# Moving two of four key and value projections from the prologue into the steps of a fused graph attention layer

## The chip, the core and the metric

The kernel runs on one core of a Trainium2 chip. The metric is the device time of one execution in microseconds (us), lower is better. TensorE (PE) multiplies, VectorE (DVE) and ScalarE (ACT) work element by element, GpSimd (POOL) adds and issues accumulating transfers, and SyncE (SP) issues most of the other transfers. Each engine works through its own instructions in their order.

## The reference, cut to what matters

Eight graphs (F) of 2048 nodes (N) with 256 channels (C) share one adjacency matrix. Every graph goes through attention with 8 heads of 32 channels, masked by the adjacency, then two layer norms around a feed-forward part, and an outer residual with a third layer norm.

```python
def layer(x, adj, w_qkv, ...):                       # x: (8, 2048, 256), adj: (2048, 2048) int32
    q, k, v = split(einsum('fnc,ck->fnk', x, w_qkv)) # 8 heads of 32 channels each
    scores = einsum('fnhd,fmhd->fhnm', q, k) / sqrt(32)
    scores = where(adj > 0, scores, -1e9)
    attn = softmax(scores, axis=-1)
    t = einsum('fhnm,fmhd->fnhd', attn, v)
    x = layernorm(x + t) * g1 + b1
    f = relu(x @ w1 + b1_) @ w2 + b2_
    return layernorm(x + f) * g2 + be2

out = layernorm(x + layer(x, adj, ...))
```

All matrix products are in float32.

## The kernel before, in words

**Tiling.** The heads are two groups (g) of four. Queries come in four chunks of 512 (qc), keys and values in 16 blocks of 128 (mb), which lie in four column chunks (c) of 512. One *item* is (f, qc, g, mb): the scores of four heads, 512 queries and 128 keys. There are 8 x 4 x 2 x 16 = 1024 items in that nesting, and the main loop in `fast_path` takes one *step* for each. In step t it first calls `advance(t)`, then records the exponential of item t+1 (L283), the scores of item t+2 (L276 on TensorE, then two adds of the mask from PSUM on VectorE, L279), and the product with the values of item t (L310). So on TensorE a step is: one piece of fill work, one group of scores, one group of values. `add_up` sums the exponentials of a query chunk on POOL, in part by additions (L339) and in part by accumulating transfers (L336).

**Fill work.** Everything else is written as generators that stop at `yield BANK` or `yield MORE` before each unit of TensorE work. `start(t, generator, due)` enters one into the list `fill`, which is kept in order of due step. `advance` resumes them by that order, as a credit for TensorE time allows; a generator past its due step goes on regardless. The fill jobs that matter here are:

- `turn(f, c)` loads a chunk of x of the next graph (L200), transposes it on TensorE (L95), and stores it to DRAM (`XD`, L205).
- `project(f, c, g)` makes the keys and values of one column chunk and one head group. It reloads the transposed chunk from `XD` (`reload`, L224) unless it is handed to it, multiplies on TensorE (L54, keys in two units, values in two), and copies the results on ScalarE (L217 and L243).
- `ask(f, c)` makes the queries of chunk c for both groups (L54, four units).
- `mask_job(n)` makes one block of the mask for query chunks 2 and 3. It loads two blocks of int32 adjacency (L156), casts them on ScalarE (L161), transposes them on TensorE (L168), encodes them on VectorE (L170), and stores the result to DRAM (L172). There are 16 such jobs; their buffers are those of one spare key and value pair and of `turned`, `hT` and `y`. `load_mask` (L179) brings mask blocks back for every query chunk.
- `denominator` (L382), `outcome`, `tail` and `feed_forward` finish a query chunk.

The tables `NEXT` and, for the first graph, `LATER` give the step within a graph at which such jobs are started. The reloads and turns share a pool of three buffers, `ld` (tile name `in`).

**Prologue.** `begin()` runs ahead of the steps. It takes the four column chunks for query chunk 0 and then for query chunk 1. For each it converts the adjacency chunk on VectorE (L696) and turns it into mask blocks (`mask_blocks`: 16 transposes on TensorE, L141, then one half copied by ScalarE, L147, the other by VectorE, L145, each stored by SP, L148). In the first four rounds it also transposes x (L95) and projects the keys and values of group 0; in the last four it projects those of group 1. In the end it records the scores of items 0 and 1:

```python
elif qc == 1:
    yield from project(0, c, 1, xT)
...
yield from mask_blocks(qc, c, cv, ...)
if (qc, c) == (1, NCK - 1):
    for k in range(LEAD):
        scores(items[k])
    exponentials(items[0])
```

The order of all instructions on every engine is fixed when the program is recorded; only waits on semaphores act at run time.

Of the kernel before, what the change touches and what calls it, by code (L numbers as in the profile page):

```python
# [61 lines left out]
def fast_path(ctx, tc, cst, x, adj, out, RS):  # L62
    nc = tc.nc
    F, N, C = x.shape
    NCK, TPC, MB = N // CH, CH // P, N // P
# [68 lines left out]
    def mask_blocks(qc, mc, cv, to=None):  # L134
        for half in range(2):
            yield BANK
            ps = bank(BF16)
            for r in range(2):
                for j in range(TPC):
                    rr = 2 * half + r  # L140
                    nc.tensor.transpose(ps[:, r, j * P:(j + 1) * P], cv[:, j, rr * P:(rr + 1) * P], identb)  # L141
            k = 2 * mc + half
            m = to[half] if to else mask_piece(0, qc, k)
            if half:
                nc.vector.tensor_tensor(m, ps, cst["ones"][:, 0:1, None].to_broadcast([P, 2, CH]), ALU.min, saturate=False)  # L145
            else:
                nc.scalar.copy(m.bitcast(I8), ps)  # L147
            nc.sync.dma_start(MD[qc, k], words(m))  # L148
# [133 lines left out]
    def exponentials(item):  # L282
        nc.scalar.activation(PT[item], PT[item], AF.Exp, scale=1.0 / math.sqrt(D))  # L283
# [371 lines left out]
    LEAD = 2  # L655
# [3 lines left out]
    def ask(f, c):  # L659
# [5 lines left out]
            60: [(project, 1, 0)], 66: [(ask, 3)], 72: [(turn, 3)], 80: [(project, 2, 0)], 98: [(ask, 0)], 100: [(project, 3, 0)],  # L665
            104: [(project, 0, 1)], 108: [(project, 1, 1)], 112: [(project, 2, 1)], 116: [(project, 3, 1)]}

    LATER = {80: [], 100: [(project, 2, 0)], 104: [(project, 3, 0)], 108: [(project, 0, 1)], 112: [(project, 1, 1)],
             116: [(project, 2, 1)], 120: [(project, 3, 1)]}

    def begin():
        todo = deque((qc, c) for qc in range(2) for c in range(NCK))
        rows, cols = [], deque()

        def fetch():
            if todo:
                qc, c = todo.popleft()
                t = pp.tile([P, 4, CH], F32, name="p").bitcast(I32)
                nc.sync.dma_start(t, adj[qc * CH:(qc + 1) * CH, c * CH:(c + 1) * CH].rearrange("(j p) m -> p j m", p=P))
                cols.append((qc, c, t))  # L680

        for c in range(NCK):
            rows.append(pp.tile([P, 4, CH], F32, name="p"))
            xc = rows[c][:, 0:2, :].rearrange("p a (b c) -> p (a b) c", c=C)
            nc.sync.dma_start(xc, x[0, c * CH:(c + 1) * CH, :].rearrange("(j p) c -> p j c", p=P))
            fetch()
        fetch()
        while cols:
            qc, c, col = cols.popleft()
            if c % 2 == 0:  # L690
                two = pp.tile([P, 4, CH], F32, name="p").rearrange("p a q -> p (a q)").bitcast(BF16)
            cv = two[:, c % 2 * TPC * CH:(c % 2 + 1) * TPC * CH].rearrange("p (j m) -> p j m", m=CH)

            for half, what in enumerate((CODE, MASKED)):
                part = slice(half * 2 * P, (half + 1) * 2 * P)
                nc.vector.tensor_scalar(cv[:, :, part], col[:, :, part], 0.0, what, op0=ALU.is_le, op1=ALU.mult)  # L696
            fetch()
            xT = rows[c][:, 2:4, :]
            if qc == 0:
                yield from turn_rows(rows[c][:, 0:2, :].rearrange("p a (b c) -> p (a b) c", c=C), xT)  # L700
                nc.sync.dma_start(XD[0][c], xT)
                XT[0, c] = xT
                if c == 0:
                    yield from queries(0, 0, xT)
                yield from project(0, c, 0, xT)
            elif qc == 1:
                yield from project(0, c, 1, xT)
            if qc and c % 2 == 0:
                out4 = take([P, 4, 2, CH], F8)
                give(out4)  # L710
            yield from mask_blocks(qc, c, cv, [out4[:, c % 2 * 2 + i] for i in range(2)] if qc else None)
            if (qc, c) == (1, NCK - 1):
                for k in range(LEAD):
                    scores(items[k])
                exponentials(items[0])

    for _ in begin():
        pass
    state["side"] = 0
    n_mask = 0  # L720
    spare.append(([kp.tile([P, CH], F32, name="kT"), vp.tile([P, TPC, P], F32, name="v").rearrange("p j c -> p (j c)")], FRAME))
    for pool, name, until in ((work, "turned", 41), (work, "hT", 41), (yp, "y", 56)):
        both = pool.tile([P, 2, CH], F32, name=name)
        spare.append(([both[:, a, :] for a in range(2)], until))
    for t, (f, qc, g, mb) in enumerate(items):
        if g == 1 and mb % 2 and (f + 1 < F or qc + 1 < NCK):
            t0 = t
            while ((qc + 1) % NCK, mb // 2) not in MADE:
                advance(t0, finish=True)
                t0 += 1  # L730
            load_mask(f + (qc + 1) // NCK, (qc + 1) % NCK, mb // 2)
        while n_mask < MB and t >= 2 + 3 * n_mask:
            start(t, mask_job(n_mask), 3 * MB - 2 + 2 * n_mask if n_mask < MB // 2 else 4 * MB - 2 + 2 * n_mask)
            n_mask += 1
        for what, *which in (NEXT if f else {**NEXT, **LATER}).get(t % FRAME, []):
            to = f if what is ask and which[0] else f + 1
            if to < F:
                at = (0, 0, 0) if what is turn else (which[0], 0, 0) if what is ask else (0, which[1], which[0] * TPC)
                start(t, what(to, *which), t + 3 * MB if what is turn else items.index((to, *at)) - LEAD - 1)
        if t == len(items) - 2 * MB - 6:  # L740
            state["xb"] = take([P, TPC, C], F32)
            nc.sync.dma_start(state["xb"], x[f, qc * CH:(qc + 1) * CH, :].rearrange("(p j) c -> p j c", p=P))
        if t == len(items) - MB:
            xr, xb = state["rows"] = [take([P, TPC, C], F32) for _ in range(2)]
            nc.sync.dma_start(xr.rearrange("p (h j) c -> p h j c", h=2),
                              x[f, qc * CH:(qc + 1) * CH, :].rearrange("(h p j) c -> p h j c", h=2, p=P))
        if t == len(items) - MB + 6:
            nc.gpsimd.tensor_tensor(xb, xr, rows(cst["be2r"]), ALU.add)
        if t:
            advance(t)  # L750

        if t + 1 < len(items):
            exponentials(items[t + 1])
        if t + LEAD < len(items):
            nf, _, ng, nmb = items[t + LEAD]
            t0 = t
# [256 lines left out]
```

## Time and profile before

| | us |
|---|---|
| median of three runs | 3171.28 |
| lowest and highest run | 3169.4 and 3172.4 |
| the profiled execution | 3170.48 |
| span of the profile | 3168.7 |
| TensorE busy | 3075.1 (97%) |
| VectorE busy | 2752.2 (87%) |
| POOL busy | 2592.1 (82%) |
| ScalarE busy | 2424.2 (77%) |
| first value product (step 0) starts at | 68.16 |
| value product of step 151 starts at | 517.53 |

The span runs from the first to the last instruction in the trace; the profiled execution's own time adds what lies around it. A busy TensorE is not one at its peak, since its instructions overlap and their ends are modelled; the start times of successive value products are the better ruler. The granted TensorE clock is 0.99 on average over the span. The timeline gives for each merged row: start, duration, engine, line, operation, tiles, count, and in brackets the idle time before it and what ended it.

### The profile page before, as it was taken

The numbers are of one execution on the slowest core, as the hardware profiler recorded it, in microseconds if no ns is written. First come the engines' busy times: TensorE is split into PE (matmuls) and PEld (weight loads), VectorE is DVE, ScalarE is ACT, GpSimd is POOL, SyncE is SP. The second block draws the span as 40 slices with busy tenths as digits, with TensorE's granted clock in tenths as the row PEclk, the third lists the DMA queues.
The fourth block names the chain that finished last, engine by engine and source line by source line (L and its number), as shares of the span: only waits on it lengthen the run. The fifth ranks groups of instructions, "written<-read, shape, count | busy, mean of one in ns | idle before, by whom it ended". The sixth has DMA issues, their size and how long they took to land.

```text
span 3168.7 us, 68994 instructions
## 1 busy us (share of the span) xinstructions
PE 3075.1 (97%) x29220; PEld 970.7 (31%) x29220; DVE 2752.2 (87%) x3138; ACT 2424.2 (77%) x1934; POOL 2592.1 (82%) x1358
## 2 busy tenths in 40 slices
PE   7999999999999999999999999999999999999986
PEld 4223233323333233323233323323233233332223
DVE  4989888988888998888988888888888888889885
ACT  4877778777778877778777878777778777778774
POOL 1768888888888888889888888888889788889885
PEclk9999999999999999999999999999999999999998
DMA  7998888888889888789878889879879788888861
GB/s 251 210 218 195 181 184 192 190 193 193 178 178 205 191 188 180 169 196 221 183 167 186 189 202 195 176 176 204 190 173 208 174 193 193 176 176 165 175 148 42
DMA packets 165467, 586.89 MB, mean 185 GB/s; under 512 B 15360, under 2 KB 84480, under 8 KB 116512
## 3 DMA queue, kind: packets, MB, share of 16 engines
q0 software_dynamic: 63696, 430.60, 68.9%
q1 hardware_dynamic: 100640, 150.50, 14.1%
q8 instruction: 231, 3.78, 0.5%
q10 hardware_dynamic: 816, 1.31, 0.1%
q14 instruction: 84, 0.69, 0.1%
HBM read 146.15 MB, written 37.75 MB: 58 GB/s over the span
## 4 chain that ended last, share of the span: by engine, by line


## 5 line engine op out<-in xcount | busy, mean ns | idle before, releaser
L279 DVE TENSOR_TENSOR p<-s,mask 128x1024 f32<-128x1024 f32 x2016 | 2371.5, 1218 | 305.9 <-PE s L276 173.4
L283 ACT ACTIVATE p<-p 128x2048 f32<-128x2048 f32 x1024 | 1955.8, 1910 | 568.4 <-DVE p L279 465.5
L339 POOL TENSOR_TENSOR p<-p 128x2048 f32<-128x2048 f32 x378 | 1846.0, 4884 | 336.7 <-ACT p L283 336.3
L276 PE MATMUL s<-qT,kT 32*128 32x512 f32 x8064 | 1154.7, 642 | 48.4 <-DVE p L279 44.5
L310 PE MATMUL x<-p,v 128*32 128x512 f32 x8064 | 1076.5, 606 | 3.5 <-ACT oT L314 3.5
L276 PEld LDWEIGHTS s<-qT,kT 32*128 32x128 f32 x8064 | 315.9, 183 | 655.6 <-DVE p L279 628.6
L336 POOL DMA_DIRECT2D p<-p x378 | 407.5, 1079 | 69.5 <-ACT p L283 41.4
L310 PEld LDWEIGHTS x<-p,v 128*32 128x32 f32 x8064 | 158.7, 108 | 770.8 <-issue 307.1
L382 PE MATMUL x<-p,halves 128*32 128x512 f32 x2016 | 261.1, 592 | 0.3 <-ACT turned L575 0.3
L54 PE MATMUL x<-in,wqkv 128*32 128x512 f32 x1888 | 245.6, 592 | 1.5 <-DVE y L170 0.8
L360 ACT ACTIVATE y<-y,nb,rs 128x256 f32<-128x256 f32 x372 | 218.3, 591 | 2.5 <-POOL nb L357 2.5
L348 DVE BATCH_NORM_STATS2 st<-y 128x6 f32<-128x256 f32 x372 | 154.9, 416 | 0.0
L54 PE MATMUL x<-turned,w1s 128*32 128x512 f32 (+1 forms) x1024 | 126.9, 593 | 0.3 <-ACT in L194 0.3
L54 PEld LDWEIGHTS x<-wqkv,in 128*32 128x32 f32 x3584 | 102.2, 110 | 62.9 <-issue 54.5
L54 PE MATMUL x<-w2s,hT 128*32 128x256 f32 x2016 | 120.3, 379 | 0.0
L54 PE MATMUL x<-wqkv,in 128*32 128x128 f32 x3584 | 117.1, 273 | 0.0
L382 PEld LDWEIGHTS x<-p,halves 128*32 128x32 f32 x2016 | 65.4, 110 | 149.8 <-issue 147.8
L54 PEld LDWEIGHTS x<-in,wqkv 128*32 128x32 f32 x1888 | 61.1, 110 | 143.4 <-issue 114.8
L354 POOL TENSOR_TENSOR rs<-rs,mhalf 128x4 f32<-128x4 f32 x93 | 96.4, 1036 | 7.8
L441 POOL TENSOR_TENSOR y<-y,g2r 128x1024 f32<-128x1024 f32 x31 | 100.5, 3241 | 0.0
L443 POOL TENSOR_TENSOR y<-y,be2r 128x1024 f32<-128x1024 f32 x30 | 92.3, 3076 | 0.6
L54 PEld LDWEIGHTS x<-w2s,hT 128*32 128x32 f32 x2016 | 65.5, 110 | 68.9 <-issue 35.6
(155 smaller groups left out, 1426.0 us busy)
## 6 DMA issues: line engine op xcount, KB each, us to landing
p<-p POOLq DMA_DIRECT2D x380, 1024.0 KB, 10.1
in<-xd SPq DMA_DIRECT2D x87, 512.0 KB, 8.5
mask<-md SPq DMA_DIRECT2D x248, 128.0 KB, 8.7
y<-in_x_dram POOLq DMA_DIRECT2D x60, 512.0 KB, 9.9
out_dram<-y SPq DMA_DIRECT2D x31, 512.0 KB, 6.2
in<-in_x_dram SPq DMA_DIRECT2D x30, 512.0 KB, 10.2
xd<-in SPq DMA_DIRECT2D x28, 512.0 KB, 8.6
p<-in_adj_dram SPq DMA_DIRECT2D x8, 1024.0 KB, 13.5
```

The costliest lines, as they stand in the source:

```text
L54: nc.tensor.matmul(out[r:r + D], lhsT[:, r:r + D], rhs, start=start, stop=stop)
L276: nc.tensor.matmul(ps2[half][:, j, :], KT[f, mb // TPC, g][r:r + D, (mb % TPC) * P:(mb % TPC + 1) * P], QT[f, qc, g][r:r + D, :], start=Tr ...
L279: nc.vector.tensor_tensor(pt[:, 2 * half:2 * half + 2, :], ps, MK[f, qc, mb // 2][:, mb % 2, None, :].to_broadcast([P, 2, CH]), ALU.add)
L283: nc.scalar.activation(PT[item], PT[item], AF.Exp, scale=1.0 / math.sqrt(D))
L310: nc.tensor.matmul(O[grp][r:r + D, :], V[f, mb // TPC, g][:, mb % TPC, r:r + D], PT[item][:, h, :], start=(mb == 0), stop=(mb == LAST))
L336: nc.gpsimd.dma_start(PT[f, qc, g, chain[0]], PT.pop(item), accum_op=ALU.add)
L339: nc.gpsimd.tensor_tensor(first, first, PT.pop(item), ALU.add)
L348: nc.vector.bn_stats(st, t[:, j, :])
L354: nc.gpsimd.tensor_tensor(rs, rs, cst["mhalf"], ALU.pow)
L360: nc.scalar.activation(t[:, j, :], t[:, j, :], AF.Identity, bias=nb[:, j:j + 1], scale=rs[:, j:j + 1])
L382: nc.tensor.matmul(ps[r:r + D, :], cst["halves"][:, g, :], term[:, h, :], start=(n == 0), stop=(n == len(blocks) - 1))
L441: nc.gpsimd.tensor_tensor(z, z, rows(cst["g2r"]), ALU.mult)
```

## The change

The change has five parts, all of which act in the first graph.

1. In the first four rounds of the prologue, the mask blocks of a chunk are recorded after the projection of the next chunk (`behind`).
2. Of the four group 1 projections, the first two stay in the prologue. Those of chunks 2 and 3 become fill jobs, started at step -6, with due steps 21 and 25.
3. The scores of items 0 and 1 and the first exponential are recorded ahead of the mask blocks of the last chunk (query chunk 1, c = 3).
4. The queries of chunk 1, `ask(0, 1)`, are started at -6 instead of step 2.
5. The due steps of the mask jobs of query chunk 3 are seven later, and the loads of its masks for the first graph are recorded eight steps later (`wanted`).

```diff
-    LATER = {80: [], 100: [(project, 2, 0)], ...
+    LATER = {2: [], 80: [], 100: [(project, 2, 0)], ...
...
                 if c == 0:
                     yield from queries(0, 0, xT)
                 yield from project(0, c, 0, xT)
-            elif qc == 1:
+                yield from behind
+                behind = mask_blocks(qc, c, cv)
+                continue
+            yield from behind
+            behind = ()
+            if c < 2:
                 yield from project(0, c, 1, xT)
-            if qc and c % 2 == 0:
+            if c % 2 == 0:
                 out4 = take([P, 4, 2, CH], F8)
                 give(out4)
-            yield from mask_blocks(qc, c, cv, [out4[:, c % 2 * 2 + i] for i in range(2)] if qc else None)
-            if (qc, c) == (1, NCK - 1):
+            yield from mask_blocks(qc, c, cv, [out4[:, c % 2 * 2 + i] for i in range(2)])
+            if c == NCK - 2:
                 for k in range(LEAD):
                     scores(items[k])
                 exponentials(items[0])
+                for k in (2, 3):
+                    start(-6, project(0, k, 1), MB + TPC * k - LEAD - 1)
+                start(-6, ask(0, 1), 2 * MB - LEAD - 1)
+                advance(-6)
...
         if g == 1 and mb % 2 and (f + 1 < F or qc + 1 < NCK):
+            wanted.append((t + (8 if (f, qc) == (0, 2) else 0), f + (qc + 1) // NCK, (qc + 1) % NCK, mb // 2))
+        while wanted and wanted[0][0] <= t:
+            _, *which = wanted.popleft()
             t0 = t
-            while ((qc + 1) % NCK, mb // 2) not in MADE:
+            while tuple(which[1:]) not in MADE:
                 advance(t0, finish=True)
                 t0 += 1
-            load_mask(f + (qc + 1) // NCK, (qc + 1) % NCK, mb // 2)
+            load_mask(*which)
         while n_mask < MB and t >= 2 + 3 * n_mask:
-            start(t, mask_job(n_mask), 3 * MB - 2 + 2 * n_mask if n_mask < MB // 2 else 4 * MB - 2 + 2 * n_mask)
+            start(t, mask_job(n_mask), 3 * MB - 2 + 2 * n_mask if n_mask < MB // 2 else 4 * MB + 5 + 2 * n_mask)
```

`advance(-6)` lets the three jobs run up to their first wait, which records their three reloads of transposed x (L224) on SP's queue. Their TensorE work follows from step 1 on. The rest of the kernel is as before.

More of the change, by code (lines that the diff above doesn't have):

```diff
@@ L666, in fast_path @@
             104: [(project, 0, 1)], 108: [(project, 1, 1)], 112: [(project, 2, 1)], 116: [(project, 3, 1)]}
-    LATER = {80: [], 100: [(project, 2, 0)], 104: [(project, 3, 0)], 108: [(project, 0, 1)], 112: [(project, 1, 1)],
+    LATER = {2: [], 80: [], 100: [(project, 2, 0)], 104: [(project, 3, 0)], 108: [(project, 0, 1)], 112: [(project, 1, 1)],
              116: [(project, 2, 1)], 120: [(project, 3, 1)]}
@@ L672, in begin @@
         todo = deque((qc, c) for qc in range(2) for c in range(NCK))
-        rows, cols = [], deque()
+        rows, cols, behind = [], deque(), ()
         def fetch():
@@ L719, in fast_path @@
     state["side"] = 0
-    n_mask = 0
+    n_mask, wanted = 0, deque()
     spare.append(([kp.tile([P, CH], F32, name="kT"), vp.tile([P, TPC, P], F32, name="v").rearrange("p j c -> p (j c)")], FRAME))
```

## The prediction

> **What bounds the kernel now.** I read the page first, then the timeline of the first 80 us, the windows around the gap I found there, the timeline step by step up to 520 us, and the DMA view of one late transfer.
>
> ```profile
> PE 3075.1 (97%) x29220; PEld 970.7 (31%) x29220; DVE 2752.2 (87%) x3138; ACT 2424.2 (77%) x1934; POOL 2592.1 (82%) x1358
> PE   7999999999999999999999999999999999999986
> ```
>
> TensorE is busy all through, except in the first slice of 79 us and at the end. The change touches only the first 520 us: in the built programs (compared by order, not run) every TensorE step from step 152 on holds the same work before and after. So I price the prologue and 151 steps.
>
> ```profile
> 54.17 1.92 PE L54 MATMUL x<-p,wqkv 128*32 128x512 f32 x16
> 55.91 1.93 PE L54 MATMUL x<-wqkv,p 128*32 128x128 f32 x64
> 57.78 1.07 PE L141 MATMUL s<-identb,p 128*128 128x128 bf16 x16
> 58.88 1.23 DVE L145 TENSOR_TENSOR in<-s,ones 128x1024 fp8e5<-128x1024 bf16 x1 [2.17 <-PE s L141]
> 60.16 1.14 PE L276 MATMUL s<-qT,kT 32*128 32x512 f32 x8 [1.32 <-DVE in L145]
> 61.42 2.35 DVE L279 TENSOR_TENSOR p<-s,mask 128x1024 f32<-128x1024 f32 x2 [1.32 <-PE s L276]
> 62.70 2.09 PE L276 MATMUL s<-qT,kT 32*128 32x512 f32 x8 [1.40 <-DVE p L279]
> 68.16 1.94 PE L310 MATMUL x<-p,v 128*32 128x512 f32 x8
> 72.04 1.07 PE L310 MATMUL x<-p,v 128*32 128x512 f32 x8
> ```
>
> These are the last quarter of the prologue and the start of the steps (columns: start, duration, engine, line, operation). The projection of one column chunk holds TensorE from 54.17 to 57.78, 3.61 us; the mask turn takes 1.0; then scores and mask adds alternate between TensorE and VectorE. The first value product (step 0) starts at 68.16, the second at 72.04. The score group of 60.16 took 1.14 us and that of 62.70 took 2.09: half clock. The windows show the clock (last three columns: granted clock, DMA share, GB/s):
>
> ```profile
> 58.85:61.85 3.00, 1.14 (x8) 0.31 (x8) 1.65 (x2) 0.59 (x1) 0.00 (x0) 1.00 0.36 93
> 61.85:72.05 10.20, 8.00 (x33) 1.76 (x34) 6.64 (x6) 5.19 (x3) 0.00 (x0) 0.50 1.08 294
> ```
>
> Three us with 1.14 us of work, and the clock is halved for 10.2 us.
>
> In the steps, the distance from one value product to the next depends on the fill work between:
>
> ```profile
> 79.56 1.07 PE L310 MATMUL x<-p,v 128*32 128x512 f32 x8
> 82.05 1.06 PE L310 MATMUL x<-p,v 128*32 128x512 f32 x8
> ...
> 87.63 1.06 PE L310 MATMUL x<-p,v 128*32 128x512 f32 x8
> 88.51 1.04 PE L54 MATMUL x<-in,wqkv 128*32 128x512 f32 x8
> ...
> 90.55 1.06 PE L310 MATMUL x<-p,v 128*32 128x512 f32 x8
> ```
>
> An empty step takes 2.49 (VectorE's two mask adds, 2 x 1.22, are the limit; TensorE's own work is 1.07 + 0.88 = 1.95). A step with one unit of projection or row sum takes 2.92: TensorE is the limit, and the unit adds 0.975. A step with a transpose of x takes 2.65. A mask turn (L168, then 1.21 on VectorE at L170) takes 2.62, and the step after it 3.26 to 3.39.
>
> One step stands out, the 32nd, 5.43 us:
>
> ```profile
> 142.24 1.58 SPq L156 DMA_DIRECT2D kT<-in_adj_dram  x1
> 159.56 0.62 ACT L161 CAST kT<-kT 128x512 bf16<-128x512 int32 x1 [2.44 <-DMA kT<-in_adj_dram]
> 162.52 0.16 PEld L310 LDWEIGHTS x<-p,v 128*32 128x32 f32 x8 [3.56 <-ACT oT L314]
> ```
>
> An adjacency load was 17.3 us on its way, ScalarE stood on its cast for 2.44 us, and the exponential, queued behind the cast, was late. The DMA view of 139.4 to 144.5 says why:
>
> ```profile
> q0 software_dynamic: 125, 1.02, 102.1%
> q1 hardware_dynamic: 231, 0.20, 12.2%
> ```
>
> POOL's accumulating transfers (q0) fill the engines while they run, and SP's loads (q1) land in bunches after them.
>
> **What the Trainium skill says.** "TensorE: Matmul & The Clock Gate", What's actually happening: an idle window of about 3.4 us halves the clock and a busy window restores it. The trace agrees with the halving (0.50 above) and needs some 5 us of work without a gap (67 to 72) to come back. "DMA: Bandwidth & Descriptors", Anatomy of one DMA: waiting is done by the issuing sequencer, so a DMA that waits holds up all behind it on its queue; the long SP gap before 100.12 shows it. Same page, Issuing engines are not separate DMA queues: all queues share the 16 engines; the 102.1% and 12.2% agree.
>
> **The change, part by part.**
>
> (1) Mask turns of the first four chunks go behind the next chunk's projection. TensorE stood still from 17.2 to 20.7 for the first adjacency block. In its place it now waits for x chunk 1, which landed at 1.78 + 19.3 = 21.07, against 22.07 when that chunk's transposes started. The 1.0 of the mask turn is paid later, partly at full clock. I take -0.3 (0 to -1).
>
> (2) Two projections leave the prologue: 2 x 3.61 = 7.2 us off TensorE. But the new order on VectorE is: mask add of quarter 2, mask adds of items 0 and 1, conversion of quarter 3 (L696), its L145, then item 2. Followed with the durations above: the turn of (1,1) ends at 49.3; L145 50.6; L696 (1.28) 51.85; second half of the turn 52.4; L145 53.7; half a score group 54.4; mask add 56.8; next 59.2; L696 60.5; half a turn, 62.1 at half clock; L145 63.4; scores of item 2 at half clock 65.5. There step 0 starts, against 68.16. TensorE works only about 1.8 of the 6.9 us from 53 on, so I take the halved clock. Step 1 then follows at 65.5 + 1.9 (values) + 1.6 (a unit, partly at half clock) + 1.1 = 70.1, against 72.04: **-1.9**. At full clock throughout it would be 66.4, -5.6; at half clock to the end 72, 0.
>
> (3) The steps. From step 1 to step 151 the kernel before took 517.53 - 72.04 = 445.5. Afterwards steps 2 to 151 hold eight units more on net (a projection is two units for keys and two for values): 8 x 0.975 = +7.8. Steps without fill are 2, 3, 4, 5, 14, 16, 23, 28 to 31 and 80 before, and 23, 28 to 31 and 76 to 79 after: three fewer, each hiding 2.49 - 1.95 = 0.54, -1.6. Taking the steps one at a time at the durations above gives another -1.3, since four mask turns in a row (steps 44 to 47, then 4.03) become three. Sum **+4.9** (1.5 to 6.5), with the 2.2 us of step 32 (5.43 against 3.26) left in.
>
> (4) SP's queue. Three loads of transposed x are now issued ahead of the last two mask stores; the third (for the queries) takes the buffer of the first and so waits until TensorE has read it for the values, in step 3 to 4, about 77.8. Queued behind it: two mask stores, all eight adjacency loads (issued at 61.6 to 68.2 before) and the next graph's x. The first adjacency load is then issued near 79.2; landing takes 5.9 with POOL quiet, 85, and ScalarE wants it before item 8's exponential, near 86.4. It just fits, cost 0 (0 to 3). Stores and mask reloads have ten steps or more; nothing.
>
> (5) The mask jobs that follow are one to five steps later. POOL's transfers around 140 to 167 keep their times, as step 20 falls at 125.9 in both. The job whose cast stood at 159.5 has successors: the load for job 8 is now issued behind the store of transposed x, which landed at 165.56, so it lands near 167.5; ScalarE wants it at 164.8. With some of that hidden by the exponential's lead I take **+2.0** (0 to 5). The later due times and the reloads of the last query chunk's masks eight steps later leave one mask that depends on a store issued near step 102 and is wanted at step 108, 17 us for a store and a load (median 8.7): 0 (0 to 3).
>
> (6) Copies for keys, values and queries move with their units; ScalarE has 0.5 to 1 us free per step there; nothing. The query projection (0,1) moves from steps 7 to 10 to 9 to 12; same price.
>
> Sum: -1.9 + 4.9 + 2.0 = **+5.0** on the profiled execution's 3170.5 us (span 3168.7), 3175.5. The median of the runs is 0.8 above the profiled time, so 3176.3.
>
> **Rivals.** A, the forecast: the saved TensorE time is largely replaced by the VectorE chain, and the units come back in the steps; +5, from -1 to +10 with the bounds of (2), (3) and (5), 3170 to 3181.
>
> B, slower: the adjacency loads. If job 8's load lands after one more of POOL's transfers (their landings are 5.5 to 7.6 apart: 153.8, 159.3, 166.9), ScalarE stands that much longer; +5.5, in all +10.5, 3182. It decides from a landing later than about 170 us. For it: loads in this stretch took 16 to 17 us already. Against it: when ScalarE stands, POOL's transfers stop too, and SP's catch up.
>
> C, faster: the clock stays full (-5.6) and the wait of step 32 goes (-2.2) with no new one: -5.6 + 4.9 - 2.2 = -2.9, and with -1 in (1), 0.7 less, and the low end of (3), 3.4 less, -7.0: 3164 to 3168. For it: the score groups break the idle time. Against it: before, 1.14 us of work in 3 us did not keep the clock.
>
> D, that the projections don't move or drift to their due times: the built order has them in steps 1 to 8; excluded.
>
> **How the numbers follow.** A 0.53, B 0.24, C 0.23. The bound of 0.2% is 6.3 us, about what a measurement of this kernel can tell. A's spread puts 0.32 within it and 0.21 above; B lies above; C puts 0.15 below and 0.08 within. Faster 0.15, same 0.40, slower 0.45: A, the likeliest case, sits just inside the bound. The range 3166 to 3186 leaves out the far ends of B and C.
>
> **What would show it.** Step 0 near 65.5 and step 1 near 70 with a clock of 0.50 before them show (2); steps 2 to 12 at 2.92 show (3); SP's third load of transposed x near 78 and the first adjacency load just behind show (4); ScalarE standing on L161 near 159 and 165 shows (5). Step 1 before 68 speaks for C, a stand of over 4 us on L161 for B. If step 151 comes with the difference of step 1 unchanged, (3) is wrong.

## The result, and the profile after

The changed kernel takes 3187.29 us in the median of six runs (3183.81 to 3189.53), the kernel before 3170.76 beside it (3168.36 to 3172.4). The ratio is 1.0054, 95% interval 1.0044 to 1.0064: slower by 17 us, where 5 were forecast. The profiled execution took 3187.07, with a span of 3185.2 against 3168.7, so +16.5.

The page hides it. Its busy times and its TensorE slices read nearly as before:

```profile
PE 3081.9 (97%) x29220; PEld 972.8 (31%) x29220; DVE 2752.4 (86%) x3138; ACT 2424.0 (76%) x1934; POOL 2591.8 (81%) x1358
PE   7899999999999999999999999999999999999986
```

Half a per cent doesn't show in 40 slices of 80 us. The ruler that shows it is the start of each step's value product (L310), step by step, in the two timelines; below, step n is the time from the value product of step n-1 to that of step n. The difference, after minus before, is +2.49 at step 0, +2.25 at step 1, +4.26 at step 7, +10.73 at step 9, +10.85 at step 31, +13.79 at step 34 and +17.31 at step 151. From there on the work is the same and 0.8 comes back by the end.

Timeline of the changed kernel, end of the prologue (start, duration, engine, line, operation, in brackets the idle time before it):

```profile
51.12 0.62 PE L141 MATMUL s<-identb,p 128*128 128x128 bf16 x8
...
55.35 3.46 PE L276 MATMUL s<-qT,kT 32*128 32x512 f32 x8
...
65.42 1.89 PE L141 MATMUL s<-identb,p 128*128 128x128 bf16 x16 [3.14 <-DVE p L696]
68.63 2.09 PE L276 MATMUL s<-qT,kT 32*128 32x512 f32 x8 [1.32 <-DVE in L145]
70.65 1.79 PE L310 MATMUL x<-p,v 128*32 128x512 f32 x8
...
74.29 1.06 PE L310 MATMUL x<-p,v 128*32 128x512 f32 x8
```

The mask turn (the transposes at L141) of query chunk 1 and column chunk 1, below (1,1), starts at 51.12 (48.58 before). From there to step 0 takes 19.53 us, against 19.58 before: no gain, although two projections have left. Its windows (TensorE busy first, granted clock third from the end) show why: the clock is halved from 55 us on.

```profile
54.00:56.00 2.00, 1.90 (x18) 1.41 (x20) 1.19 (x3) 1.01 (x1) 0.00 (x0) 0.77 0.22 72
...
60.00:64.00 4.00, 2.09 (x8) 0.52 (x8) 2.87 (x4) 1.91 (x1) 0.00 (x0) 0.50 0.31 126
```

The largest loss is between steps 7 and 9. Timeline of the changed kernel, SP's queue:

```profile
57.09 25.39 SPq L224 DMA_DIRECT2D in<-xd  x3
82.53 0.90 SPq L148 DMA_DIRECT2D md<-in  x2
83.47 0.49 SPq L156 DMA_DIRECT2D kT<-in_adj_dram  x1
```

The three reloads form one row of 25 us: the third is issued only at 82.16, two mask stores follow, and the first adjacency load leaves at 83.47. The view of SP's waits (us in total, times, longest) names what held the third, TensorE's last read of the first reload's buffer (L54, which ends in step 4):

```profile
SPq L224 <- PE x L54: 21.3, 1, 21.3
```

POOL issues its first accumulating transfer just ahead of that load, and the next at 84.89 (first the kernel before, then the changed one):

```profile
81.12 1.83 POOL L336 DMA_DIRECT2D p<-p  x2
...
83.32 0.93 POOL L336 DMA_DIRECT2D p<-p  x1
84.89 0.87 POOL L336 DMA_DIRECT2D p<-p  x1 [0.65 <-ACT p L283]
```

The DMA view from 83.3 to 97.3 us (packets, MB and share of the engines for each queue, then KB and us to landing) and the timelines of ScalarE and TensorE:

```profile
q0 software_dynamic: 280, 2.09, 72.2%
q1 hardware_dynamic: 1257, 1.19, 29.8%
...
kT<-in_adj_dram SPq DMA_DIRECT2D x1, 256.0 KB, 13.8
```

```profile
97.30 0.62 ACT L161 CAST kT<-kT 128x512 bf16<-128x512 int32 x1 [6.84 <-DMA kT<-in_adj_dram]
```

```profile
91.89 1.06 PE L310 MATMUL x<-p,v 128*32 128x512 f32 x8
...
99.78 1.93 PE L310 MATMUL x<-p,v 128*32 128x512 f32 x8 [4.88 <-ACT p L283]
```

The load lands after 13.8 us, ScalarE stands (waits) on its cast for 6.84, the exponential behind the cast is late, and step 8 (from the value product of step 7 at 91.89 to its own at 99.78) takes 7.89 instead of 2.92. TensorE's clock falls at the end of the wait, so step 9 takes 4.43 instead of 2.93.

### The profile page after: what moved, and what is told of

Its sections match the earlier page's. It is cut to its first block, busy times and chain, and to the rows that moved or that the text cites. A ratio compares the mean times of both kernels' runs of the same rounds, so it can differ in the third digit from the quotient of the medians.

```text
span 3185.2 us, 69002 instructions
## 1 busy us (share of the span) xinstructions
PE 3081.9 (97%) x29220; PEld 972.8 (31%) x29220; DVE 2752.4 (86%) x3138; ACT 2424.0 (76%) x1934; POOL 2591.8 (81%) x1358
## 3 DMA queue, kind: packets, MB, share of 16 engines
q8 instruction: 231, 3.78, 0.5%
## 4 chain that ended last, share of the span: by engine, by line
## 5 line engine op out<-in xcount | busy, mean ns | idle before, releaser
L310 PE MATMUL x<-p,v 128*32 128x512 f32 x8064 | 1077.8, 607 | 9.4 <-ACT p L283 5.3
L310 PEld LDWEIGHTS x<-p,v 128*32 128x32 f32 x8064 | 158.7, 108 | 776.1 <-issue 310.9
L54 PE MATMUL x<-in,wqkv 128*32 128x512 f32 x1920 | 250.4, 594 | 0.9 <-DVE hT L170 0.8
L54 PE MATMUL x<-turned,w1s 128*32 128x512 f32 (+1 forms) x1008 | 125.6, 593 | 0.0
L54 PEld LDWEIGHTS x<-wqkv,in 128*32 128x32 f32 x3712 | 105.7, 110 | 65.1 <-issue 55.4
L54 PE MATMUL x<-w2s,hT 128*32 128x256 f32 x2048 | 122.0, 379 | 0.0
L54 PE MATMUL x<-wqkv,in 128*32 128x128 f32 x3712 | 121.1, 273 | 0.1
L54 PEld LDWEIGHTS x<-in,wqkv 128*32 128x32 f32 x1920 | 62.4, 110 | 146.5 <-issue 120.1
L54 PEld LDWEIGHTS x<-w2s,hT 128*32 128x32 f32 x2048 | 66.4, 110 | 69.7 <-issue 35.3
```

Of the source, the lines that this page charges most:

```text
L54: nc.tensor.matmul(out[r:r + D], lhsT[:, r:r + D], rhs, start=start, stop=stop)
L310: nc.tensor.matmul(O[grp][r:r + D, :], V[f, mb // TPC, g][:, mb % TPC, r:r + D], PT[item][:, h, :], start=(mb == 0), stop=(mb == LAST))
```

## The experiments

Times are given as ratios to the kernel before, run on the same chip beside each of them; 0.0010 is 3.2 us. Times inside a run are from one profiled execution.

### The third reload on SP's queue

**Moved by two places** (part 4 undone).

```diff
-    LATER = {2: [], 80: [], 100: ...
+    LATER = {80: [], 100: ...
...
-                start(-6, ask(0, 1), 2 * MB - LEAD - 1)
```

> The changed kernel with one DMA moved: the third reload of transposed x (for the queries) is recorded in step 2, behind the last two mask stores, instead of ahead of them; no other instruction of the main loop changes its place on any engine. Theory (the reload waits for TensorE's read of the first reload's buffer, the eight adjacency loads stand behind it on SP until 83.5 us, and then meet POOL's accumulating transfers): the adjacency loads issue before 75 us and land within 7 us, no stand on L161 before item 8, step 8 takes about 2.9 us instead of 7.9 and step 9 about 2.9 instead of 4.4; the time falls by 6.5 us, to about 3181 (5 to 8 less). Rival 1 (loads at this place are slow because of POOL's transfers whenever they are issued): the loads are issued early but land late, L161 still stands over 3 us, 0 to 2 us less. Rival 2 (the excess is TensorE's halved clock alone): no change.

Measured: 1.0032 (1.0020 to 1.0044), against 1.0054: about 7 us less. In its timeline the reload waits 1.4 us instead of 21.3, and the first four of the eight adjacency loads go with POOL quiet; the DMA view from 69 to 78 us gives the landing of the first:

```profile
69.20 0.32 SPq L224 DMA_DIRECT2D in<-xd  x1
69.56 0.44 SPq L156 DMA_DIRECT2D kT<-in_adj_dram  x1
```

```profile
kT<-in_adj_dram SPq DMA_DIRECT2D x1, 256.0 KB, 3.9
```

Steps 8 and 9 take 2.94 and 2.93. Theory held. A wait of one DMA, not work, cost over a third of the loss. Behind the mask stores the reload takes another buffer, whose last user is a mask store of the prologue and not TensorE:

```profile
SPq L224 <- DMA md<-in: 1.4, 1, 1.4
```

**POOL's transfers taken away instead.**

```diff
-                nc.gpsimd.dma_start(PT[f, qc, g, chain[0]], PT.pop(item), accum_op=ALU.add)
+                moved = PT.pop(item)
+                if item[:3] != (0, 0, 0):
+                    nc.gpsimd.dma_start(PT[f, qc, g, chain[0]], moved, accum_op=ALU.add)
```

> The changed kernel without the accumulating transfers of POOL for the first group of 16 items (8 transfers; the softmax sums of that group lack those terms). SP's order is kept, so the first adjacency load is still issued at about 83.5 us. Theory (it lands late only because POOL's transfers fill the DMA engines): it lands 5 to 7 us after its issue, near 90 us, instead of 13.8; ScalarE's stand on L161 falls from 6.8 us to 0 to 1.5, the difference of step 9 to the kernel before from 10.7 to 4 to 6 us, and the time by 5 to 7 us. Rival (the loads are late through their issue alone, or fill the DMA engines themselves, eight at once): landing still 11 us or more, L161 stands over 4 us, the time falls by less than 2.5 us.

Measured: 1.0034 (1.0022 to 1.0046). SP's block is still there (the load is issued at 81.82), yet the DMA view from 81.5 to 90 us shows

```profile
kT<-in_adj_dram SPq DMA_DIRECT2D x1, 256.0 KB, 5.0
```

and ScalarE doesn't stand on L161. So both are needed: the late issue and POOL's transfers. Either one taken away removes the stand of steps 8 and 9.

### The projections, the early scores and the clock

**Early scores alone** (part 3 in the kernel before).

```diff
-            if (qc, c) == (1, NCK - 1):
+            if (qc, c) == (1, NCK - 2):
```

> The kernel before with part 3 alone: the scores and mask adds of the first two items stand ahead of the last mask quarter; all eight projections stay in the prologue. Theory: TensorE has the last projection (3.6 us) to do while VectorE adds the masks, so TensorE's clock holds longer than in the changed kernel and VectorE's chain (four mask adds, two conversions, L145, two mask adds) sets the end; step 0 starts 16 to 18 us after the mask turn of (1,1), against 19.6 in the kernel before and 19.5 to 19.9 in the changed kernel, and no unit is added to the steps: 2 to 3 us less, about 0.999 of before. Rival (the chain is as long whatever TensorE does, since the clock falls in it): 19.5 us again, no change.

Measured: 0.9991 (0.9985 to 0.9998), 3166.26 us, so about 3 us less. This version is faster than both kernels. Its windows and its first steps:

```profile
54.00:56.00 2.00, 1.14 (x8) 0.31 (x8) 1.34 (x2) 0.15 (x1) 0.00 (x0) 1.00 0.36 121
...
60.00:64.00 4.00, 3.74 (x78) 2.61 (x71) 2.77 (x4) 2.84 (x4) 0.00 (x0) 1.00 0.01 4
```

```profile
64.86 1.06 PE L310 MATMUL x<-p,v 128*32 128x512 f32 x8
...
67.33 1.07 PE L310 MATMUL x<-p,v 128*32 128x512 f32 x8
```

The clock stays at 1.00 in this execution. From the mask turn of (1,1) at 47.88, step 0 comes after 16.98 us and step 1 after 19.45 (before: 19.58 and 23.46). The last projection, which the change moves away, runs here from 57.82 to 61.4 beside VectorE's mask adds.

**Moved projections alone** (part 2).

```diff
-            elif qc == 1:
+            elif c < 2:
...
                 exponentials(items[0])
+                for k in (2, 3):
+                    start(-6, project(0, k, 1), MB + TPC * k - LEAD - 1)
+                advance(-6)
```

> The kernel before with part 2 alone: the projections of chunks 2 and 3 (keys and values of the second four heads) are done between the steps; mask turns and scores keep their places, and the reload for the queries stands behind the mask stores. Theory: eight units come back in the steps (+5.6 us by step 151, of that +2 in steps 2 to 7), the stand of ScalarE on later adjacency loads near steps 32 to 35 adds 3 to 4, and the prologue gives back only what VectorE's conversions leave, 0 to 3.5 us: +5 to +9, about +7. Rival (the prologue's end is set by TensorE, so that both projections' 7.2 us come off): +2 or less.

Measured: 1.0026 (1.0015 to 1.0036), 8 us slower, in the expected range, but in part by another way. The prologue gives 16.0 us from the mask turn to step 0, 3.6 less than before, and 20.8 to step 1, 2.6 less. The steps take it back: +2.0 from step 1 to 7 and +4.4 in steps 32 to 35, as expected. What follows was not: at step 95 a mask had not been made when its reload was due, and that step took 11.93 instead of 3.78, so that +6.5 came from step 35 to 151.

**Clock held in the chain.** TensorE is given transposes of the unit matrix in its waits, with the reload behind the stores.

```diff
+    awake = {(1, 2, 0): 26, (1, 3, 0): 34}
...
             ps = bank(BF16)
+            for i in range(awake.get((qc, mc, half), 0)):
+                nc.tensor.transpose(ps[:, 0, 0:P], identb, identb)
...
+        for i in range({(0, 0, 0, 1): 9, (0, 0, 0, 2): 9}.get(item, 0)):
+            nc.tensor.transpose(ps2[1][:, 0, 0:P], ident, ident)
```

> The changed kernel with the third reload behind the mask stores (as in the run of that name), and with 60 small transposes of the unit matrix (bf16) and 18 of the f32 one in TensorE's waits of the score chain (ahead of the mask turns of (1,2) and (1,3) and of the scores of items 1 and 2), whose results are overwritten; they take about 1.7 to 2.3 us a wait at full clock. Theory (the halved clock costs the chain its gain): granted clock 0.9 or more from the mask turn of (1,1) to step 1, step 0 starts 16.5 to 17.8 us after that turn, against 19.85 without them, step 1 follows after 3.0 to 3.9 instead of 4.9, and the time falls by 2.5 to 4 us against the run without them. Rival (VectorE sets the chain, the clock is incidental): 19.3 to 19.9 us again, at most 1 us less.

Measured: 1.0026 (1.0017 to 1.0035), and 20.13 us to step 0. It missed its aim: the transposes ahead of item 1's scores wrote into a bank that VectorE still read, so they waited with the scores (1.38 us), the clock fell at 58.9 us, and the later ones ran at half clock (3.04 us for 34). It says nothing on the question.

**Clock held**, with transposes into a bank that is free.

```diff
+    awake = {(1, 2, 0): 26, (1, 3, 0): 40}
...
+        if item in ((0, 0, 0, 1), (0, 0, 0, 2)):
+            spin = ps_x[1].tile([P, CH], F32, name="x1")
+            for i in range(16 if item[3] == 1 else 10):
+                nc.tensor.transpose(spin[:, 0:P], ident, ident)
```

> The changed kernel with the third reload behind the mask stores, and transposes of the unit matrix in TensorE's four waits of the score chain: 26 (bf16) ahead of the mask turn of (1,2), 16 (f32) ahead of the scores of item 1, 40 (bf16) ahead of the mask turn of (1,3), 10 (f32) ahead of the scores of item 2; those ahead of scores go into a PSUM bank that nothing else uses then, so that they start at once. Their results are not used. Theory (without the two projections TensorE has too little to do in the chain, its clock halves, and that takes back what the early scores give): granted clock 1.00 up to step 1, step 0 starts 16.5 to 17.8 us after the mask turn of (1,1) (19.85 without them), step 1 after another 2.9 to 3.2 (4.9), so step 1 comes 3.5 to 5 us earlier after that turn; the time falls by 3 to 5 us against the run without them. Rival (VectorE sets the chain and the clock is incidental): 19 to 20 us to step 0, less than 1.5 us in the time.

Measured: 1.0016 (1.0010 to 1.0023), against 1.0032 without: about 5 us less. Window and first two value products (at L318 in this kernel):

```profile
60.00:64.00 4.00, 3.15 (x34) 2.24 (x34) 2.40 (x3) 2.71 (x2) 0.00 (x0) 1.00 0.10 35
```

```profile
64.25 1.07 PE L318 MATMUL x<-p,v 128*32 128x512 f32 x8
...
67.17 1.07 PE L318 MATMUL x<-p,v 128*32 128x512 f32 x8
```

From the mask turn at 47.88 that is 16.37 us to step 0 and 19.29 to step 1; without the transposes 19.85 and 24.77. VectorE's work is the same in both. So the halved clock takes back what parts 2 and 3 give.

**Mask turns in place, reload behind the stores** (the old order of part 1 with the other parts).

```diff
-                yield from behind
-                behind = mask_blocks(qc, c, cv)
-                continue
...
-                start(-6, ask(0, 1), 2 * MB - LEAD - 1)
```

> The changed kernel without part 1 and with the third reload behind the mask stores: projections moved, scores ahead of the last mask quarter, later due times. Theory: the two effects add, no stand in steps 8 and 9; 6.4 us less than the changed kernel for the reload and 0 to 2.5 for the mask turns, so 1.0025 to 1.0034 of before. Rival (the stand of steps 8 and 9 moves to another load): 1.004 or more.

Measured: 1.0026 (1.0015 to 1.0036), as expected; no stand in steps 8 and 9. Step 0 comes 17.54 us after the mask turn.

**The same with the scores at the end.**

```diff
-            if (qc, c) == (1, NCK - 2):
+            if (qc, c) == (1, NCK - 1):
```

> As the run above (projections moved, later due times, mask turns in place, third reload behind the mask stores), but with the scores of the first two items behind the last mask quarter, as in the kernel before. Theory (the early scores give nothing once the projections are gone): step 0 starts about 16 us after the mask turn of (1,1), step 1 about 20.8, that is no later than with the scores ahead (17.5 to 19.9, and 21.4 to 24.8), so the time is the same as of the run above or up to 3 us less. Rival (the early scores are worth 2 us or more also here): 2 us or more above it.

Measured: 1.0023 (1.0013 to 1.0033), so the same within 3 us; 16.56 us to step 0 and 21.38 to step 1 (17.54 and 21.36 with the scores ahead). With the projections gone, the early scores give nothing that these runs can tell. Each of the parts 2 and 3 shortens the prologue alone; together they don't add.

### The order of the mask turns

**Part 1 alone.**

```diff
+                yield from behind
+                behind = mask_blocks(qc, c, cv)
+                continue
+            yield from behind
+            behind = ()
```

> The kernel before with part 1 alone: the mask turns of the first four chunks go behind the next chunk's projection, all else stays. Theory (TensorE starts its first long work at 21.9 us from idle at half clock and stays at half clock to about 27, and the mask turn comes after it): the mask turn of chunk (1,1) starts about 2.5 us later than before (51.1 against 48.6), the first value product at about 70.7 against 68.2, the time rises by 2.5 us (1.5 to 3). The prediction's step (1): 0.3 us less (0 to 1 less). Rival (the later adjacency blocks or VectorE's conversions take up the delay): the start is later but the first value product is within 0.7 us of 68.2.

Measured: 1.0006 (0.9998 to 1.0015), 1.9 us slower, with an interval that reaches zero. But in its profiled execution the mask turn of (1,1) starts at 47.82 and step 0 at 67.41, earlier than before.

**Part 1 undone in the changed kernel.**

```diff
-                yield from behind
-                behind = mask_blocks(qc, c, cv)
-                continue
-            yield from behind
-            behind = ()
```

> The changed kernel without part 1: each mask turn stands directly behind its own chunk's projection again, as before; all else is kept. Theory: the mask turn of (1,1) is back near 48.6 us, the first value product near 68.1 (70.65 in the changed kernel), and the time falls by 2.5 us (1.5 to 3.5). The prediction's step (1): 0.3 us more (0 to 1). Rival (the score chain behind it absorbs the difference by another clock): the first value product between 69.5 and 71, less than 1 us of change.

Measured: 1.0052 (1.0039 to 1.0066), 0.6 us less than the changed kernel, where the intervals leave room for some 5 us either way. In the profiled execution step 0 is at 64.72, the stand on L161 comes one step later (6.73 and 5.28 for steps 9 and 10).

Both profiled executions contradict their medians, so I set the mask turn of (1,1) beside the clock of 21 to 28 us in all fourteen executions that have no added transposes ahead of it:

| order of mask turns | clock 1.00 from 21 to 28 us | half clock from 21 to 23 us on |
|---|---|---|
| old | 47.2, 47.9 | 48.6, 48.6, 49.1, 49.6; 1.00 again by 25 |
| new | 47.8, 47.9, 47.9 | 49.6, 50.0, 51.1, 51.3, 51.5; 1.00 again at 26 to 28 |

The start of that turn is a draw: it depends on whether the clock falls in this stretch, which it does with either order. Where it stays full, the two orders start within 0.8 us of each other, in too few executions to tell more; where it falls, the new order costs 1.7 more (means 50.7 and 49.0). A difference of 2.5 between two executions is then no measure of the order.

**Part 1 with the clock held.**

```diff
-    def turn_rows(xc, xT):
+    def turn_rows(xc, xT, spin=0):
...
             ps = bank()
+            for i in range(spin):
+                nc.tensor.transpose(ps[:, 0:P], ident, ident)
+            spin = 0
             transposes(ps, [xc[:, j, a * P:(a + 1) * P] for j in range(TPC)])
```

> The kernel before with part 1 alone, and 30 f32 transposes of the unit matrix on TensorE ahead of the transposes of x chunk 1 (the wait from 17 to 21 us), overwritten by those. Theory (part 1 costs only through the half clock from 21 to 27 us, which begins in that wait in most executions): granted clock 1.00 from 17 to 31 us, the mask turn of (1,1) at 47.6 to 48.2 us, the time 1 to 2.5 us below the run of part 1 alone, so 0.9998 to 1.0004 of before. Rival (the order itself delays TensorE): that turn at 49 us or later and no less time.

Measured: 1.0013 (1.0007 to 1.0020), above the 1.0006 of part 1 alone, with intervals that overlap. The clock is 1.00 from 17 to 64 us, the mask turn comes at 48.45 (the transposes of x start at 21.80, behind the added ones, against 21.14 in the run of part 1 alone), step 1 is 1.07 earlier than before. All of it and more is lost in steps 32 and 33, which take 10.29 and 4.85 instead of 5.43 and 2.92: ScalarE stands 7.31 us on an adjacency load, which is issued at 142.25 (142.24 in the kernel before) and lands at 163.35 instead of 159.54. The time did not confirm the theory; the clock and the start agree with it within 0.3 us.

### The later adjacency loads and the due times

**POOL's second group of transfers taken away**, with the reload behind the stores.

```diff
+                if item[:3] != (0, 0, 1):
+                    nc.gpsimd.dma_start(PT[f, qc, g, chain[0]], moved, accum_op=ALU.add)
```

> The changed kernel with the third reload behind the mask stores, and without POOL's accumulating transfers for the second group of 16 items (8 transfers; the softmax sums of that group lack those terms). Theory (step (5): the loads of the later mask jobs land late because of these transfers): the loads issued between 140 and 170 us land within 8 us, L161 no longer stands before steps 32 to 35, step 32 takes 2.9 to 3.4 instead of 5.5 and steps 34 and 35 together 5.9 to 6.5 instead of 9.8, so the time falls by 5 to 6.5 us against the run with them. Rival (the loads are issued too late because SP stands on the store of transposed x): steps 34 and 35 still take over 8 us together, 2.5 us less at most.

Measured: 1.0007 (1.0001 to 1.0014), against 1.0032: about 8 us less. Steps 32 to 35 take 11.8 together, where the run with the transfers took 18.2 and the kernel before 14.2. The DMA views, first of the changed kernel from 154 to 169 us, then of this run from 142 to 154:

```profile
y<-in_adj_dram SPq DMA_DIRECT2D x2, 256.0 KB, 16.1
kT<-in_adj_dram SPq DMA_DIRECT2D x1, 256.0 KB, 11.8
```

```profile
y<-in_adj_dram SPq DMA_DIRECT2D x2, 256.0 KB, 3.2
kT<-in_adj_dram SPq DMA_DIRECT2D x1, 256.0 KB, 3.6
```

**Part 5 undone**, with the reload behind the stores.

```diff
-            wanted.append((t + (8 if (f, qc) == (0, 2) else 0), ...
+            wanted.append((t, ...
...
-            start(t, mask_job(n_mask), ... else 4 * MB + 5 + 2 * n_mask)
+            start(t, mask_job(n_mask), ... else 4 * MB - 2 + 2 * n_mask)
```

> The changed kernel with the third reload behind the mask stores and without part 5 (due times of the second eight mask jobs and the mask reloads of the last query chunk as before). Up to step 64 nothing differs. Theory (the eight added units push the mask jobs back, so that one mask is not made when its reload is due, and all fill work is forced in one step): one step near 95 takes 8 us or more and the following two or three are short by 1 each, 4 to 7 us more than the run without this edit. Rival (the later due times are themselves what the steps from 86 to 151 lose, 3.5 us): 2 to 4 us less.

Measured: 1.0041 (1.0027 to 1.0055), against 1.0032: 3 us more, less than the 4 to 7 expected. Step 95 does take 13.43 instead of 2.92, with the second feed-forward unit of that wait at half clock:

```profile
359.53 3.42 PE L54 MATMUL x<-w2s,hT 128*32 128x256 f32 x32 [1.38 <-DVE kT L170]
```

The two profiled executions differ ahead of that too, where the edit changes nothing: at step 64 this run is 1.7 us ahead of the one with part 5, by steps 32 to 35. From there it loses 6.9 to step 99 and 4.3 to step 151, since units that were forced at step 95 are no longer due later. So the size fits the expectation in these executions, and the ratios can't tell 3 from 4. Part 5 is a repair that the moved units need.

### The faster version with its clock held

```diff
             ps = bank(BF16)
+            for i in range(50 if (qc, mc, half) == (0, 0, 0) else 0):
+                nc.tensor.transpose(ps[:, 0, 0:P], identb, identb)
```

> The kernel before with part 3 alone, and 50 bf16 transposes of the unit matrix ahead of the first mask turn (TensorE's wait from 17 to 21 us), overwritten by it. Theory: granted clock 1.00 from 17 us to step 1 in every execution, so that the time falls by the 1 to 1.5 us that the half clock from 21 to 24 us costs in some executions: 0.5 to 1.5 us below the run of part 3 alone, 0.9984 to 0.9990 of before. Rival (that wait is covered by the adjacency blocks and VectorE later on): the same as part 3 alone.

Measured: 0.9995 (0.9987 to 1.0004), not below the 0.9991 without; the intervals overlap. Step 1 comes 4.84 us earlier than in the kernel before, at a full clock, but the profiled execution of the early scores alone had a full clock too and came 4.71 earlier. And steps 32 to 35 take 18.0 instead of the 14.3 of that run, since the loads for them meet POOL's transfers at another phase: one of them is issued at 139.2 in both and lands at 160.27 instead of 155.62. In their profiled executions both versions that held the first clock lost time there. The early scores alone have the lowest ratio of all runs.

## Why the prediction was wrong

Mechanism by mechanism, in the profiled executions:

| step of the prediction | forecast | measured | from |
|---|---|---|---|
| (1) mask turns behind | -0.3 | +2.5 | 51.12 - 48.58; about +1.9 (-0.6 to 4.8) by the run of part 1 alone |
| (2) shorter chain | -1.9, with the -0.3 of (1) in it | -0.3 | step 1: +2.25, of which 2.54 is (1) |
| (3) units in the steps | +4.9 | +5.6 | +2.0 steps 2 to 7, +0.1 from 9 to 31, +3.5 from 35 to 151 |
| (4) SP's queue | 0 (0 to 3) | +6.5 | steps 8 and 9: 4.26 to 10.73 |
| (5) later mask jobs | +2.0 (0 to 5) | +2.9 | steps 32 to 34: 10.85 to 13.79 |
| sum | +5.0 | +17.3 | step 151; +16.5 in the span |

**(4) is the step that failed most.** Its first half was right: the reload behind the read of the first buffer, the mask stores and loads queued behind it, ScalarE's cast as the place where it would show. It said 77.8 for the reload; it was 82.2, because step 1 came at 74.29 and not at 70.1. What failed is the cost of the landing: the text used the 5.9 us measured "with POOL quiet" for a load issued near 79 to 83, and so put the term at 0; the load took 13.8, and steps 8 and 9 lost 6.5. Yet the trace of before had POOL's first accumulating transfers issued at 81.12 and 81.86. A duration was taken from one traffic and used in another, on the very engines whose contention the same text had shown at 142 us. The late start of the steps is no excuse: POOL's first transfer comes 9.1 us behind step 1 before (81.12 - 72.04) and 9.0 after (83.32 - 74.29), so with step 1 at 70.1 it would have come near 79.2, just where the text put the load. Rival B named the mechanism (a load behind one more of POOL's transfers), but placed it at job 8 near step 32. With the 16 to 17 us that loads took beside POOL's transfers at 142, the load would have landed near 96 and not 85, some 9 us after ScalarE wants it, and the upper bound of (4) would have been 9 and not 3.

**(2) had the right chain and the wrong clock.** Where the clock stays full up to the second scores, the chain takes 17.54 us (the two runs with parts 2 and 3 and the mask turns in place); the prediction's own sum gives 17.2 from the same turn. It let the clock fall after 59 us. In the five executions with the mask turns behind and nothing added to the chain it fell at 51 to 55, 3.4 to 4.2 us after that turn began and shortly behind the wait of 1.9 us that the moved projection had filled, and the chain took 19.4 to 19.9. Its bound "0 at half clock to the end" held. The sentence that was missing is that the removed work was itself the cover of the clock: TensorE's 3.6 us of projection beside VectorE's mask adds keep it at 1.00, as the two executions with part 3 alone show, and added transposes in its place do the same.

"TensorE: Matmul & The Clock Gate", What's actually happening, says that the window by which the clock is set runs freely, so that the moment of a change varies. The runs agree: one order of instructions gave both 47.9 and 51 us. The traces also show the window. In each of the sixteen, the changes of the granted clock lie on one grid of 3.41 us (kernel before: 20.91, 24.33, 61.88, 72.11, which are 1, 11 and 3 times 3.41 apart), and the place of the grid differs from execution to execution. The place of the grid separates the two cases behind the turn. In the five executions above, the whole wait of 1.92 us lies in one interval of the grid, TensorE is busy for about 1.5 us of it, and the clock falls at its end. In the two with the mask turns in place the same wait is split between two intervals, and the clock falls only at the end of the interval behind them, 9.1 to 9.2 us after the turn. The two runs with the moved projections and the scores at the end agree: the clock fell at once where the wait lay whole in one interval (52.0 us), and one interval later where it was split (55.4 us). First the changed kernel, then the one with the reload behind the stores:

```profile
51.67:55.08 3.41, 1.49 (x25) 1.17 (x23) 2.42 (x3) 1.44 (x3) 0.00 (x0) 1.00 0.24 83
...
48.55:51.96 3.41, 2.15 (x60) 1.78 (x49) 1.23 (x3) 1.59 (x3) 0.00 (x0) 1.00 0.35 119
51.96:55.37 3.41, 2.49 (x22) 1.41 (x24) 2.43 (x4) 1.01 (x1) 0.00 (x0) 1.00 0.29 99
55.38:58.79 3.41, 2.03 (x12) 0.39 (x10) 2.35 (x2) 0.01 (x1) 0.00 (x0) 1.00 0.78 266
```

So the interval ahead of a fall need not be idle as a whole. How much work in it is enough stays open: 2.03 us of busy TensorE were too little here, and the run of the moved projections alone kept the clock with 1.57 (48.56 to 51.97).

**(1) failed** because it priced the turn of 1.0 us and the landing of x, not the clock. First the kernel before, then the changed one:

```profile
20.68 1.71 PE L141 MATMUL s<-identb,p 128*128 128x128 bf16 x16 [3.45 <-DVE p L696]
...
21.92 1.94 PE L95 MATMUL s<-ident,p 128*128 128x128 f32 x8 [4.67 <-DMA p<-in_x_dram]
```

TensorE waits 4.67 us for x where it waited 3.45 for the adjacency block. The clock falls about as often as with the old order (five of eight executions, four of six), but it comes back later (27.78 instead of 24.33 in these two), with the long work of the projection now in front of the turn. The +2.5 of the profiled execution is partly such a draw; how much of it the median holds is not settled beyond 0 to 5 us.

**(3) held**, 0.7 above its value, within its range. **(5) held** in its mechanism, size and place:

```profile
171.24 0.62 ACT L161 CAST y<-y 128x512 bf16<-128x512 int32 x1 [3.27 <-DMA y<-in_adj_dram]
179.68 0.62 ACT L161 CAST kT<-kT 128x512 bf16<-128x512 int32 x1 [3.21 <-DMA kT<-in_adj_dram]
```

ScalarE stands on L161 for 3.27 and 3.21 us where it stood 2.44 and 1.86 (the latter hidden), and the load for job 8 lands at 179.65, behind POOL's transfer that lands at 178.22. Without POOL's transfers it vanishes. The text let those transfers keep their times; they came some 11 us later, with the steps. **(6)**: no copy shows as a wait on the path.

Rival C, faster, asked for a full clock and no wait. The run with held clock and the reload moved had a full clock up to step 1, and was still 5 us slower than before, by (3) and (5). The moved work left a prologue in which TensorE is not the limit and came back, as 5.6 us for eight units, in steps in which TensorE has little to spare.

## What to carry to other kernels

Before work is moved off an engine, ask what it covers: here the moved projection kept the clock up under another engine's chain, and 5.6 us came back in steps where TensorE has little to spare. A landing time belongs to the traffic around it; when a change delays a load, look up in the trace what else is on the DMA engines at the new time. And a prologue whose clock may or may not fall is judged by many runs or by starts measured from the same event, not by two executions.

## What the hardware showed

- A load of 256 KB on SP's queue landed after 3.9 us when issued at 69.56 with POOL quiet (the run with the reload moved), and after 13.8 when issued 0.15 us behind an accumulating transfer of POOL (the changed kernel). In the run with the reload moved, two more loads issued at 82.62 and 83.18, ahead of POOL's first transfer at 83.39, took 5.7 and 5.9; the next two, at 83.73 and 84.28, took 15.4 and 21.2. Here the order within one microsecond decided.
- The same load can cost more when all is earlier. Two runs that reached step 31 4.8 and 1.1 us earlier than the kernel before lost 3.8 and 6.8 us more than it in steps 32 to 35, since their loads met POOL's transfers at another phase. The early scores alone reached it 4.7 us earlier and lost nothing there, so a lead alone doesn't cost.
- TensorE's clock changed only on a grid of 3.41 us, placed differently in each execution. Behind one and the same wait of 1.92 us it fell where the wait lay whole in one interval of the grid (six executions) and not at that point where it was split between two (three executions). To come back it needed 3.65 us of gapless work in the kernel before (20.68 to 24.33) and 5.86 of nearly gapless work in the changed one (21.92 to 27.78).
